# Moving projections, values and the first steps of cross attention between the eight units of a group

## The chip, the cores and the metric

The kernel runs on one core of a Trainium2 chip. The core has five engines, each with its own queue of instructions, which it works off in order: TensorE (PE, with its weight loads listed as PEld), VectorE (DVE), ScalarE (ACT), GpSimd (POOL) and SyncE (SP, which here only issues DMAs). They meet through semaphores alone. The metric is the device time of one execution in microseconds; the kernel before took 3197.55 us, the median of three runs (3197.34 to 3203.16).

## The reference

Input x is 64 sequences of 128 positions and 256 features in fp32, and so is a context. Two decoder layers run one after the other, each of three residual sublayers behind a layer normalization:

```
x = x + mamba(norm(x))                     layer 0: state space mixer
x = x + cross_attention(norm(x), context)  16 heads, rotary positions
x = x + recurrence(norm(x))                gated recurrence over the 64 sequences
x = x + self_attention(norm(x))            layer 1: 16 query heads, 4 key heads, RMS norm inside
x = x + cross_attention(norm(x), context)  one head 256 wide, no output projection
x = x + experts(norm(x))                   8 experts, 2 chosen per position, and a shared one
```

The change lies in the fourth and fifth lines. Self attention there is

```
q = (xn @ w_q) * rf;  k = (xn @ w_k) * rf;  v = xn @ w_v
s = softmax(q k^T / 16) v                  per head of 16
x = x + s + s @ w_o
```

and the cross attention is softmax((xn Wq + bq)(ctx Wk + bk)^T / 16) (ctx Wv + bv), one 128 x 128 score matrix for each sequence.

## The kernel before, in words

The 64 sequences stay in SBUF as 16 groups of four (X[g], 128 positions x 4 x 256). Four stages follow each other: layer 0's mixer; its cross attention with the recurrence; layer 1's two attentions with the routing of the experts; the experts. The change is in the third stage, which runs in the profile from about 1800 to 2735 us.

The order of that stage is written out. Each piece of work is a Python generator (`self_inputs`, `self_attention`, `cross_and_route`) and `run_units` (line 65) steps them: a step has a unit number and a priority, steps run by unit, then by priority, then by their place in the task list, and `yield du, p` says that the next step is du units later with priority p. The order in which steps emit instructions is the order in which PE, VectorE, ScalarE and GpSimd execute them (`manual_schedule(engines=PINNED)`); SyncE's DMAs are ordered by the framework. Units are no clock: a unit is only a stretch of each engine's queue, and an engine may be ahead of another.

One group takes eight units, and everything below repeats with that period, so a unit is known by its number modulo 8 (u0 to u7).

- **Self attention proper** (`attention`, line 241, priority 0 to 8 by step) has one step for each sequence b and half of the heads c, eight for a group, beginning at unit 8g+11. Two units after it begins PE makes the scores s (line 257, two matmuls on two halves of the array into the buffers s0 and s1), VectorE takes the minimum mx of each (L263), ScalarE makes the exponentials e with their sums (L275, four for s0, and at priority 4 four for s1). A unit later PE transposes e (pt, L287), ScalarE copies the first half to eT (L289) and VectorE the second (L291), and at priority 8 PE multiplies with the values (av, L305). After the second half of the heads follow, in odd units, the reciprocal sums (rd, L296 and L312), and in even units the copy prs (L317), their product oT (L320) and the output projection pr (L324), added to X by VectorE (L328) one unit on. The scores of half c wait until the exponentials have read that buffer in the unit before.
- **`self_inputs(g)`** begins at unit 8g, priority 5: load of the recurrence's output xo, addition (L739), tanh (L741), addition to X (L743, GpSimd), statistics (L194 to L198, their reciprocal root on GpSimd, L182), two factors (L749 to L754), the normalized xn on ScalarE (L208), its transposes (L220, copied to xnT by ScalarE, L222, and VectorE, L224), the three projections to q, q and k (L234, multiplied with the rotary factors by VectorE, L764) and the values pv (L242, copied by ScalarE, L774).
- **`cross_and_route(g)`** begins at unit 8g+24, priority 5: `wide_attention` is the cross attention: load of the context (L570), statistics, xn, values(0) of the first two sequences (L242, bias added by VectorE, L803), transposes, two projections (L234, copied by ScalarE, L815, with two products called junk on VectorE, L817), scores (L826), reductions (L830), values(2) of the other two sequences, exponentials (L838), transposes (L846), the copy eT2 (L848), the product po (L853) and its addition to X (L858). `route` follows one unit later: a third normalization (xnr), its transposes, two stores of xnT to DRAM (L872), the gate's logits pl (L242), ranks (L882 to L896), counts pc (L901) and places (L905 to L927), and eight indirect DMAs that scatter the rows (L931, GpSimd, priority 6).

Steps of priority 5 of three different groups share each unit with one step of attention. They stand after the attention's exponentials and before its pr and av.

PSUM has eight buffers of 128 x 512: one each for s0, s1, pt0, pt1 and av, and three ("mm") that all other matmul results take in turn. In SBUF xn and the context's tile have one buffer each (`xn` is shared by self and cross attention), xnT has two, q and k two.

Of the kernel before, what the change touches and what calls it, by code (L numbers as in the profile page):

```python
# [41 lines left out]
def mid(ap, n):  # L42

    return ap.unsqueeze(1).to_broadcast([ap.shape[0], n, ap.shape[1]])
# [34 lines left out]
def tile_decoder(ctx: ExitStack, tc: tile.TileContext, a: dict, out: bass.AP):  # L79
    nc = tc.nc  # L80
    B = a["x"].shape[0]
    NG = B // G
# [131 lines left out]
    def transposed(work, ps, xn, bufs=2):  # L214

        xnT = [work.tile([P, T], F32, tag=f"xnT{c}", name=f"xnT{c}", bufs=bufs) for c in range(2)]
        for c in range(2):
            pt = ps.tile([P, T], F32, tag="mm", name="pt_ln")
            for b in range(G):
                nc.tensor.transpose(pt[:, b * P:(b + 1) * P], xn[:, b, c * P:(c + 1) * P], ident)  # L220
            if c == 0:
                nc.scalar.copy(xnT[c], pt)  # L222
            else:
                nc.vector.tensor_copy(xnT[c], pt)  # L224
        return xnT

    def halves(t):
        return [t[:, c, :] for c in range(2)]
# [101 lines left out]
    def values_of(work, n, i):  # L330

        v = work.tile([P, n, 64], F32, tag=f"v{i}", name=f"v{i}")
        nc.gpsimd.memset(v[:, :, 16:48], 0.0)
        return v

    def pairs(v):

        return v.rearrange("p n (f e) -> p n f e", e=16)[:, :, 0:4:3, :]
# [194 lines left out]
    with phase_pool("work1", "left") as work, phase_pool("ps1", space=PSUM) as psp:  # L533
        ps = PsumPool(psp, {"mm": 6, "seg": 1})
        got = {}
# [21 lines left out]
    def scale_weights():  # L557
        nc.gpsimd.tensor_scalar_mul(fuo, fuo, 0.5)
        for c in range(2):
            for w in (lwq, lwk, lwv):  # L560
                nc.gpsimd.tensor_scalar_mul(w[:, c, :], w[:, c, :], lg[:, c:c + 1])

            wd = lwo[:, c, c * P:(c + 1) * P]
            nc.gpsimd.tensor_tensor(out=wd, in0=wd, in1=ident, op=ALU.add)
        nc.gpsimd.tensor_scalar_mul(lwq, lwq, -1.0 / 16)
        yield 1, 6
# [135 lines left out]
    with phase_pool("work2", "left") as work, phase_pool("ps2", space=PSUM) as psp:  # L702
        ps = PsumPool(psp, {"mm": 3, "s0": 1, "s1": 1, "pt0": 1, "pt1": 1, "av": 1})
        got = {"c2": c2, "v": [values_of(work, 8, i) for i in range(3)]}
        rows = [(g, b) for g in range(NG) for b in range(G)]
        tasks = [(40, 6, scale_weights())]
# [27 lines left out]
    ATTEND = 13  # L734

    def self_inputs(g, work, ps, hc, got):
        xo = work.tile([P, G, D], F32, tag="xo", name="xo")
        nc.sync.dma_start(out=xo, in_=XO[g])
        nc.gpsimd.tensor_tensor(out=xo, in0=xo, in1=mid(hc, G), op=ALU.add)  # L739
        yield 1, 5  # L740
        nc.scalar.activation(xo, xo, AF.Tanh)  # L741
        yield 1, 5
        nc.gpsimd.tensor_tensor(out=X[g], in0=X[g], in1=xo, op=ALU.add)  # L743
        yield 1, 5
        mv, rstd = start_norm(g, work)
        yield 1, 5

        ms = work.tile([P, G], F32, tag="ln_ms", name="ln_ms", bufs=2)
        nc.vector.tensor_tensor(ms, rstd, rstd, ALU.mult)  # L749
        nc.vector.tensor_tensor(ms, ms, mv[:, :, 1], ALU.mult)  # L750
        nc.vector.tensor_scalar(ms, ms, RMS_EPS, None, ALU.add)
        inv = power(work, "ln_inv", ms)
        yield 1, 5
        nc.vector.tensor_tensor(inv, inv, rstd, ALU.mult)  # L754
        xn = end_norm(g, work, mv, inv, "xn")
        yield 1, 5
        xnT = transposed(work, ps, xn)
        yield 1, 5
        qT = work.tile([P, 2, T], F32, tag="qT", name="qT", bufs=2)
        kT = work.tile([P, T], F32, tag="kT", name="kT", bufs=2)  # L760
        for c in range(3):
            pp = project(ps, lwq if c < 2 else lwk, c * P if c < 2 else 0, P, xnT)
            dst = qT[:, c, :] if c < 2 else kT
            nc.vector.tensor_tensor(  # L764
                dst.rearrange("p (b t) -> p b t", b=G), pp.rearrange("p (b t) -> p b t", b=G),
                mid(rfT, G), ALU.mult,
            )
            if c > 0:
                yield 1, 5
        pv = ps.tile([P, T], F32, tag="mm", name="pv")  # L770
        for b in range(G):
            project_rows(pv[:, b * 64:(b + 1) * 64], xnT, lwv, b)
        v = got["v"][g % 2]
        nc.scalar.copy(pairs(v), pv[:, :D].rearrange("p (n f e) -> p n f e", f=2, e=16))  # L774
        got[g] = qT, kT, v
# [15 lines left out]
    def wide_attention(g, work, ps):  # L791
        ctx_tile = load_ctx(work, g, 1)
        cT = halves(ctx_tile)
        mv, rstd = start_norm(g, work)
        yield 1, 5
        xn = end_norm(g, work, mv, rstd, "xn")
        v = work.tile([P, G, D], F32, tag="v2", name="v2")

        def values(b):
            pv = ps.tile([P, 2, D], F32, tag="mm", name="pv")  # L800
            for i in range(2):
                project_rows(pv[:, i, :], cT, ywv, b + i)
            nc.vector.tensor_tensor(v[:, b:b + 2, :], pv, mid(ybv, 2), ALU.add)  # L803

        values(0)
        yield 1, 5
        xnT = transposed(work, ps, xn)
        yield 1, 5
        qT = work.tile([P, 2, T], F32, tag="qT2", name="qT2")

        qb = work.tile([P, G], F32, tag="qb2", name="qb2", bufs=2)
        junk = work.tile([P, D], F32, tag="junk2", name="junk2")
        for c in range(2):
            pp = project(ps, ym, c * P, P, xnT)
            nc.scalar.activation(qT[:, c, :], pp, AF.Identity, bias=ymb[:, c:c + 1])  # L815
            for b in range(2 * c, 2 * c + 2):
                nc.vector.scalar_tensor_tensor(  # L817
                    junk, xn[:, b, :], 1.0, yu[:, :D], ALU.mult, ALU.mult, accum_out=qb[:, b:b + 1]
                )
            yield 1, 5  # L820
        nc.vector.tensor_scalar(qb, qb, yu[:, D:D + 1], None, ALU.add)
        s = ps.tile([P, G, P], F32, tag="mm", name="s")
        for b in range(G):
            tb = slice(b * P, (b + 1) * P)
            for k in range(2):
                nc.tensor.matmul(  # L826
                    s[:, b, :], lhsT=qT[:, k, tb], rhs=cT[k][:, tb], start=(k == 0), stop=(k == 1)
                )
        mx = work.tile([P, G], F32, tag="mx2", name="mx2", bufs=2)
        nc.vector.tensor_reduce(mx, s, AX.X, ALU.min)  # L830

        nc.vector.tensor_tensor(mx, mx, qb, ALU.add)
        nc.vector.tensor_tensor(mx, mx, qb, ALU.subtract)
        values(2)
        e = work.tile([P, G, P], F32, tag="e2", name="e2")
        den = work.tile([P, G], F32, tag="den2", name="den2", bufs=2)
        for b in range(G):
            nc.scalar.activation(  # L838
                e[:, b, :], s[:, b, :], AF.Exp, bias=mx[:, b:b + 1], scale=-1.0,
                accum_out=den[:, b:b + 1],  # L840
            )
        yield 2, 5
        nc.vector.reciprocal(den, den)
        pt = ps.tile([P, G, P], F32, tag="mm", name="pt")
        for b in range(G):
            nc.tensor.transpose(pt[:, b, :], e[:, b, :], ident)  # L846
        eT = work.tile([P, G, P], F32, tag="eT2", name="eT2")
        nc.scalar.copy(eT, pt)  # L848
        yield 1, 5
        for b in range(0, G, 2):  # L850
            po = ps.tile([P, 2, D], F32, tag="mm", name="po")
            for i in range(2):
                nc.tensor.matmul(  # L853
                    po[:, i, :], lhsT=eT[:, b + i, :], rhs=v[:, b + i, :], start=True, stop=True
                )
            for i in range(2):
                xb = X[g][:, b + i, :]
                nc.vector.scalar_tensor_tensor(  # L858
                    xb, po[:, i, :], den[:, b + i:b + i + 1], xb, ALU.mult, ALU.add
                )  # L860
        yield 1, 5
# [76 lines left out]
    def cross_and_route(g, work, ps, got):  # L938
        yield from wide_attention(g, work, ps)
        yield from route(g, work, ps, got)  # L940

    with phase_pool("work3", "left") as work, phase_pool("ps3", space=PSUM) as psp:
        ps = PsumPool(psp, {"mm": 3, "s0": 1, "s1": 1, "pt0": 1, "pt1": 1, "av": 1})
# [36 lines left out]
        nc.vector.tensor_tensor(hc, ph[:, :D], fbo, ALU.add)  # L980
        got = {"full": base, "v": [values_of(work, G * 2, i) for i in range(2)]}
        tasks = [(8 * g, 5, self_inputs(g, work, ps, hc, got)) for g in range(NG)]
        tasks += [(8 * g + ATTEND + 11, 5, cross_and_route(g, work, ps, got)) for g in range(NG)]
        tasks += [
            (8 * g + ATTEND - 2 + 2 * b + c, 0, self_attention(g, b, c, work, ps, got))
            for g in range(NG) for b in range(G) for c in range(2)
# [7 lines left out]
    with phase_pool("work4", "left") as work, phase_pool("ps4", space=PSUM) as psp:  # L994
        ps = PsumPool(psp, {"mm": 5, "dn": 3})
# [307 lines left out]
```

## Time and profile before

| | |
|---|---|
| median of three runs | 3197.55 us |
| the profiled execution | 3206.84 us, its span 3205.1 us |
| TensorE matmuls busy | 2996.5 us, 93% |
| TensorE weight loads busy | 2047.4 us, 64% |
| VectorE busy | 1972.3 us, 62% |
| ScalarE busy | 1861.5 us, 58% |
| GpSimd busy | 1262.5 us, 39% |
| granted TensorE clock, mean | 0.966 |
| from 1840 to 2680 us: PE, VectorE, ScalarE busy | 814.7, 619.5, 639.7 of 840 us |

How to read the lines that follow. A line of the timeline has the start in us, the length in us, the engine, the line of the code, the operation, what it writes and reads by the program's names, the tile's shape and how many instructions were merged; a bracket at its end tells how long the engine was idle before and what ended that. A fp32 matmul stands there as two instructions. Lengths of PE rows overlap, since a matmul's record runs on while the next is under way, so PE's pace is read from one start to the next. A line of the table by stretches has the stretch, its length, then the busy time of PE, PEld, VectorE, ScalarE and GpSimd with the number of instructions, the granted clock, the share of DMA and GB/s. The last line of the page's fourth part ranks engines by their share of the chain of waits that ended last.

### The profile page before, as it was taken

The page shows a single profiled execution, that of the slowest core. Times are in us where ns is not written, and L with a number is a line of the kernel's source. Part 1 is how long each engine was busy: PE and PEld are TensorE (multiplying, and loading weights), DVE is VectorE, ACT ScalarE, POOL GpSimd, SP SyncE. Part 2 cuts the span into 40 slices and gives each one's busy share as a digit, 9 for nine tenths or more (in the row PEclk, how much of TensorE's full clock was granted, in tenths as well). Part 3 has the DMA queues.
Part 4 walks back from the last instruction along what each step waited for, and adds up shares of the span by engine and source line. Part 5 has one row for each costly group of instructions (what it writes and reads, how often), then busy time and mean ns, then how long its engine had stood idle before and what let it go on. Part 6 is the DMA issues. An engine that isn't in the chain of part 4 may idle for free.

```text
span 3205.1 us, 54587 instructions
## 1 busy us (share of the span) xinstructions
PE 2996.5 (93%) x19022; PEld 2047.4 (64%) x19022; DVE 1972.3 (62%) x4955; ACT 1861.5 (58%) x6693; POOL 1262.5 (39%) x1204
## 2 busy tenths in 40 slices
PE   7999999996999999999999699999999997899587
PEld 4565555553777777777777456666666664688354
DVE  6887887773555555555555357777878774433344
ACT  4555555553777666766776377777787873233100
POOL 3444444453434433333332222434252422333564
PEclk9999999997999999999999899999999997899888
DMA  9990000001111111111110100111111111677453
GB/s 303 342 342 31 1 1 1 1 15 42 41 32 31 40 34 31 32 39 36 29 33 21 43 14 27 59 42 60 41 60 40 54 37 59 204 222 222 129 164 120
DMA packets 192196, 246.59 MB, mean 77 GB/s; under 512 B 24624, under 2 KB 156208, under 8 KB 191920
## 3 DMA queue, kind: packets, MB, share of 16 engines
q1 hardware_dynamic: 173952, 196.92, 19.9%
q0 software_dynamic: 17968, 46.18, 4.7%
q8 instruction: 150, 2.46, 0.3%
q14 instruction: 126, 1.03, 0.1%
HBM read 113.65 MB, written 127.93 MB: 75 GB/s over the span
## 4 chain that ended last, share of the span: by engine, by line
PE 75%; ACT 8%; DVE 6%; issue 4%; POOL 2%; another core or an unknown queue 1%; DMA 1%; SPq 1%; DVEq 0%; POOLq 0%; ACTq 0%
PE proj L234 18%; PE s L257 9%; PE pt L287 6%; PE pu L664 5%; PE pu L660 5%; PE av L305 4%; ACT e L275 3%; PE po L516 3%; PE seg L484 3%; PE pv L242 2%; PE pr L324 2%; PE pgu L1112 2%; PE py L501 2%; PE pxo L242 2%; PE pd L1175 2%
## 5 line engine op out<-in xcount | busy, mean ns | idle before, releaser
L275 ACT ACTIVATE e<-s,mx 128x128 f32<-128x128 f32 x2048 | 740.3, 395 | 384.6 <-DVE mx L263 384.6
L263 DVE TENSOR_REDUCE mx<-s 128x4 f32<-128x512 f32 x512 | 331.6, 685 | 465.2 <-PE s L257 455.3
L275 ACT ACTIVATION_READ_ACCUMULATOR e<-s,mx 128x1 f32 x2048 | 476.3, 233 | 0.0
L182 POOL TENSOR_TENSOR ln_rstd<-ln_ve,neghalf 128x4 f32<-128x4 f32 x80 | 82.1, 1026 | 685.2 <-DVE ln_ve L198 555.5
L257 PE MATMUL s<-kbd,qT 64*128 64x512 f32 x1024 | 334.5, 652 | 18.5 <-POOL qT L600 8.6
L287 PEld LDWEIGHTS pt<-consts,e 128*128 128x128 f32 x2048 | 223.0, 142 | 196.5 <-issue 151.0
L234 PE MATMUL proj<-xnT,win 128*128 128x512 f32 x640 | 298.9, 611 | 16.0 <-DVE xc L397 16.0
L287 PE MATMUL pt<-consts,e 128*128 128x128 f32 x2048 | 284.1, 282 | 0.0
L660 PE MATMUL pu<-xnTb,fx 128*128 128x128 f32 x1536 | 235.6, 276 | 1.2 <-DVE xnTb L651 1.2
L664 PE MATMUL pu<-c,fu 128*128 128x128 f32 x1536 | 234.5, 275 | 1.8 <-DVE c L695 1.8
L660 PEld LDWEIGHTS pu<-xnTb,fx 128*128 128x128 f32 x1536 | 208.0, 192 | 31.3 <-issue 23.9
L234 PEld LDWEIGHTS proj<-xnT,win 128*128 128x128 f32 x640 | 119.9, 194 | 147.7 <-issue 115.0
L407 DVE SCALAR_TENSOR_TENSOR acc<-proj,convw,acc 128x508 f32<-128x508 f32 (+2 forms) x288 | 207.0, 735 | 8.3 <-ACT acc L403 7.3
L342 POOL TENSOR_TENSOR kbd<-kT,consts 128x512 f32<-128x512 f32 x192 | 202.8, 1066 | 5.3 <-PE s L257 4.7
L664 PEld LDWEIGHTS pu<-c,fu 128*128 128x128 f32 x1536 | 202.3, 192 | 2.4 <-DVE c L695 2.4
L291 DVE COPY eT<-pt 128x512 f32<-128x512 f32 x256 | 174.9, 683 | 7.4 <-PE pt L287 7.4
L305 PE MATMUL av<-eT,v 128*32 128x128 f32 x4096 | 165.8, 280 | 13.3 <-ACT eT L289 13.3
L506 POOL TENSOR_TENSOR y<-y,zs 128x512 f32<-128x512 f32 x64 | 81.4, 1271 | 230.9 <-DVE y L505 223.1
L599 POOL TENSOR_TENSOR other<-other,consts 128x512 f32<-128x512 f32 x64 | 81.4, 1272 | 198.7 <-DMA other<-raw 198.7
L1136 POOL DMA_INDIRECT ys<-ys,t_yrow x128 | 124.7, 975 | 87.9 <-DVE x L1148 38.3
L305 PEld LDWEIGHTS av<-eT,v 128*32 128x32 f32 x4096 | 96.7, 109 | 96.1 <-issue 31.4
L289 ACT COPY eT<-pt 128x512 f32<-128x512 f32 x256 | 155.6, 608 | 2.9 <-PE pt L287 2.7
(277 smaller groups left out, 6432.4 us busy)
## 6 DMA issues: line engine op xcount, KB each, us to landing
xs<-zeros SPq DMA_DIRECT2D x64, 1024.0 KB
xs<-xs SPq DMA_DIRECT2D x71, 256.0 KB
ys<-y SPq DMA_DIRECT2D x71, 256.0 KB
ctxT<-in_ctxT_dram SPq DMA_DIRECT2D x32, 512.0 KB
other<-raw SPq DMA_DIRECT2D x256, 64.0 KB
x<-in_x_dram SPq DMA_DIRECT2D x16, 512.0 KB
xo<-xo SPq DMA_DIRECT2D x64, 128.0 KB
xo<-xo SPq DMA_DIRECT2D x16, 512.0 KB
```

The lines of the kernel that those rows point to most:

```text
L234: nc.tensor.matmul(o[:m, :], lhsT=w[:, k, m0:m0 + m], rhs=rhs[k], start=(k == 0), stop=(k == 1))
L257: nc.tensor.matmul(ss[i], lhsT=q()[rows], rhs=kb[rows, :, :], start=True, stop=True)
L263: nc.vector.tensor_reduce(mx[i], ss[i], AX.X, ALU.min)
L275: nc.scalar.activation(e[i][:, h, :], ss[i][:, h, :], AF.Exp, bias=mx[i][:, h:h + 1], scale=-1.0, accum_out=den[:, at:at + 1],)
L287: nc.tensor.transpose(pt[:, h, :], e[i][:, h, :], ident)
L289: nc.scalar.copy(eT[i], pt)
L291: nc.vector.tensor_copy(eT[i], pt)
L305: nc.tensor.matmul(av[j * 32:j * 32 + 32, c, :], lhsT=values(h), rhs=eT[h // 4][:, h % 4, :], start=(odd == 0), stop=(odd == 1),)
L342: nc.gpsimd.tensor_tensor(out=kb, in0=mid(k, 4), in1=last(mask, P), op=ALU.mult)
L407: nc.vector.scalar_tensor_tensor(acc[:, :, k:], pv[:, :, :P - k], convw[:, c, 3 - k:4 - k], acc[:, :, k:], ALU.mult, ALU.add,)
L660: nc.tensor.matmul(pu[:, i, :], lhsT=fx[:, k, m], rhs=xnT[:, k, :], start=(k == 0), stop=False)
L664: nc.tensor.matmul(pu[:, i, :], lhsT=fu[:, k, m], rhs=got["c2"][:, k, :], start=False, stop=(k == 1),)
```

## The change

Three things move; no operation is added or taken out.

- In `self_inputs` the first projection is followed by a step's end like the other two, so that the four pieces (three projections, values) lie in units 7, 8, 9 and 10 of the group; they lay in 7, 7, 8 and 9.
- In `wide_attention` values(0) stands behind the transposes of xn in the following unit; it stood in the unit of the normalization. values(2) stands in a unit of its own between the exponentials and the transposes of e; it stood before the exponentials, and the unit between had nothing of this piece.
- `cross_and_route` begins at unit 8g+25; it began at 8g+24. Its length in units is unchanged.

```diff
@@ self_inputs, in the loop over the three projections
-            if c > 0:
-                yield 1, 5
+            yield 1, 5
@@ wide_attention, after the normalization
+        yield 1, 5
+        xnT = transposed(work, ps, xn)
         values(0)
-        yield 1, 5
-        xnT = transposed(work, ps, xn)
         yield 1, 5
@@ wide_attention, after the reductions of the scores
-        values(2)
         e = work.tile([P, G, P], F32, tag="e2", name="e2")
         ...
-        yield 2, 5
+        yield 1, 5
+        values(2)
+        yield 1, 5
         nc.vector.reciprocal(den, den)
@@ the list of tasks
-        tasks += [(8 * g + ATTEND + 11, 5, cross_and_route(g, work, ps, got)) for g in range(NG)]
+        tasks += [(8 * g + ATTEND + 12, 5, cross_and_route(g, work, ps, got)) for g in range(NG)]
```

More of the change, by code (lines that the diff above doesn't have):

```diff
@@ L803, in values @@
             nc.vector.tensor_tensor(v[:, b:b + 2, :], pv, mid(ybv, 2), ALU.add)
-        values(0)
         yield 1, 5
         xnT = transposed(work, ps, xn)
+        values(0)
         yield 1, 5
```

## The prediction

> **What bounds the kernel now.** I read the page first (the chain that ended last), then busy time by unit, then each engine's order of work inside one group. On the chain TensorE has three quarters, so a gain has to come out of TensorE's own time.
>
> ```profile
> PE 75%; ACT 8%; DVE 6%; issue 4%; POOL 2%; another core or an unknown queue 1%; DMA 1%; SPq 1%; DVEq 0%; POOLq 0%; ACTq 0%
> ```
>
> The changed code repeats once a group. The context load, one a group, gives the period, 52.9 us; twelve groups (units 32 to 127) have it within 0.2 us.
>
> ```profile
> 2194.28 0.38 SPq L570 DMA_DIRECT2D ctxT<-in_ctxT_dram  x1
> 2247.16 0.38 SPq L570 DMA_DIRECT2D ctxT<-in_ctxT_dram  x1
> ```
>
> Busy time in the eight units of one group, cut where each unit's score matmuls start. I call them u1 to u7 and u0, unit number modulo 8, in the order of the rows.
>
> ```profile
> core 0: us, PE busy (x) PEld busy (x) DVE busy (x) ACT busy (x) POOL busy (x), PEclk, DMA share, GB/s
> 2162.55:2169.09 6.54, 6.54 (x58) 4.93 (x54) 6.42 (x26) 4.05 (x20) 2.64 (x3) 1.00 0.02 4
> 2169.09:2174.69 5.60, 5.15 (x41) 3.10 (x40) 3.77 (x6) 5.60 (x20) 4.93 (x5) 1.00 0.13 47
> 2174.69:2181.13 6.44, 6.44 (x46) 3.54 (x42) 5.45 (x17) 6.44 (x27) 3.56 (x4) 1.00 0.43 123
> 2181.13:2188.58 7.45, 7.45 (x53) 5.02 (x53) 4.12 (x16) 5.91 (x25) 5.42 (x6) 1.00 0.35 125
> 2188.58:2195.12 6.54, 6.54 (x58) 4.93 (x55) 5.13 (x12) 4.59 (x21) 4.39 (x4) 1.00 0.06 20
> 2195.12:2200.36 5.24, 4.73 (x42) 3.09 (x41) 3.70 (x9) 5.24 (x26) 0.00 (x0) 1.00 0.37 100
> 2200.36:2208.48 8.12, 8.12 (x50) 4.38 (x46) 6.36 (x19) 5.55 (x25) 0.00 (x0) 1.00 0.01 2
> 2208.48:2215.44 6.96, 6.96 (x45) 4.46 (x44) 6.21 (x23) 3.77 (x18) 0.00 (x0) 1.00 0.00 0
> ```
>
> PE looks full, but ScalarE is full in exactly the units u2, u3 and u6. The order inside shows what that costs:
>
> ```profile
> 2169.09 1.13 PE L257 MATMUL s<-kbd,qT 64*128 64x512 f32 x4
> 2171.97 0.77 PE L220 MATMUL pt_ln<-consts,xn 128*128 128x128 f32 x5 [0.16 <-ACT xn L208]
> 2174.12 0.64 PE L305 MATMUL av<-eT,v 128*32 128x128 f32 x16 [0.24 <-ACT eT L289]
> 2174.69 1.96 PE L257 MATMUL s<-kbd,qT 64*128 64x512 f32 x4
> ```
>
> The score matmuls use two halves of the array side by side and take 1.06 us from their start to the next group's. Where the second half waits for the last exponentials of the unit before, they run one after the other (1.96): +0.83, counted as busy. The reason is ScalarE's queue:
>
> ```profile
> 2168.85 1.11 ACT L741 ACTIVATE xo<-xo 128x1024 f32<-128x1024 f32 x1
> 2169.81 2.10 ACT L208 ACTIVATE xn<-x,ln_off,ln_rstd 128x256 f32<-128x256 f32 x4
> 2172.03 0.42 ACT L275 ACTIVATE e<-s,mx 128x128 f32<-128x128 f32 x1
> 2175.27 2.16 ACT L208 ACTIVATE xnr<-x,ln_off,ln_rstd 128x256 f32<-128x256 f32 x4
> ```
>
> In u1 a tanh and a normalization stand behind the exponentials, so those of u2 begin 2.94 us into their unit; in u1 they began 2.49 in, and with ScalarE and VectorE free it is 1.94 (u5: 2190.53 less 2188.58).
>
> **PE's own work per unit**, from start-to-start times of this group's PE timeline: scores 1.06, transposes of e 0.93, av 0.57; even units add pr 0.96, odd ones the transposes of rd 0.37. So 3.52 even, 2.93 odd. Inputs: a 512-column projection 1.72 to 1.80, pv of self attention 1.74, values 1.85, po 1.72, pl 1.71, cross scores 1.79, a normalized input's transposes 0.90, cross pt 0.56, pc 0.37.
>
> Before, u0 to u7: 6.96, 6.54, 4.40, 5.62, 7.03, 6.54, 4.45, 7.29; sum 48.83. Measured 52.89: **4.06 us a group are stall**, at u2 1.20, u3 0.83, u4 0.41, u6 0.79, u7 0.83. The largest gain is thus 12 x 4.06 = 49 us, some 54 with the partial groups.
>
> **The change, part by part.** No instruction is added or removed; matmuls, evacuations and DMAs stay as many. What counts is which unit each falls in.
>
> Self attention: the projections lie in u7, u0, u1 (were u7, u7, u0), pv in u2 (was u1). Cross attention and routing start one unit later; values(0) goes behind the transposes (now u3), values(2) behind the exponentials, a unit of its own (u7).
>
> PE after: u0 3.52+1.72+0.37+0.56 = 6.17; u1 2.93+1.72+1.72 = 6.37; u2 3.52+1.74 = 5.26; u3 2.93+0.90+1.85 = 5.68; u4 3.52+0.87+1.75 = 6.14; u5 2.93+1.71+1.80 = 6.44; u6 3.52+0.90+1.79 = 6.21; u7 2.93+1.72+1.85 = 6.50. Sum 48.8.
>
> ScalarE's inputs (tanh 0.96, a normalization 1.97, copy of xnT 0.47, qT 0.58, four cross exponentials 1.37, eT2 0.55, v 0.25): before 0, 3.18, 2.44, 1.05, 0.83, 3.34, 0.47, 0.55; after 0.55, 0.96, 2.22, 2.44, 1.05, 2.80, 1.84, 0. The two heaps of u1+u2 (5.62) and u5 (3.34) become 3.18 and 2.80. Its attention part is 3.24 even, 3.56 odd.
>
> VectorE, whole units: before 6.87, 4.70, 2.80, 5.45, 3.60, 4.20, 5.60, 6.00; after 5.25, 7.03, 3.96, 5.32, 4.11, 3.53, 3.71, 6.34. This is less even: po's adds 1.57, the cross statistics 1.79, the placing 0.79 and kT 0.61 all fall in u1, now only 6.37 long.
>
> Walking the units with these: exponentials start at the latest of 1.94 us, the first reduction + 0.78, and ScalarE's free time; the next unit starts after PE's work, and not before exponentials + 2.67 (even) or 3.04 (odd), since av waits for eT. For the kernel before this gives the rows above: u2 2.94 + 2.67 = 5.61 against 5.60. After: u7, u0 and u1 are PE's own work. In u1 VectorE starts its reductions at 1.16, works 2.27 + 4.76 and waits 0.5 for kT's projection, 8.66, so u2's first reduction starts at 2.29, the exponentials at 3.07, and u2 lasts 5.74 (**stall 0.48**). Its normalization ends ScalarE's work 2.79 into u3; scores serial 0.83, transposes wait 0.1: u3 lasts 6.61 (**stall 0.93**). ScalarE ends u3's exponentials at 6.35, before u4 begins, so u4 to u7 are PE's work. Sum 50.2: **-2.7 a group, -32 over twelve**.
>
> Edges: the two lighter groups at units 24 to 31 and 128 to 135 lose part of these stalls (-1.6, -2.4), units 16 to 23 -0.5. In the drain PE runs values(0) (2.71 there) behind the transposes and no longer while it waits for xn: +2; VectorE's ranking of the group before no longer stands behind the add of values(2): -2. The start of attention, 8g+11, is unmoved. Together -36.
>
> Costed at nothing, and what hides it. *ctxT*: its one buffer is free after values(2), now in u7 and not u5, and is read in u3. From the load's issue to values(0) that was 24.9 us (2166.28 + 52.9 less 2194.28) and becomes 0.9 + 6.17 + 6.37 + 5.74 + 3.8 = 23.0; the xo load queued behind it on SyncE waits for u2 anyway. Were 512 KB not there in 23 us, u3 would be longer by the lateness; no row shows such a wait. *xnT's two stores* go one unit later; nobody reads them before the last stage. *GpSimd*: the reciprocal root of the cross statistics now waits for u1's late VectorE and holds up the X addition (2.36), the routing root and the scatters behind it; the X addition then ends near 5.8 in u2 and is wanted 3.7 into u3, 3.6 us of cover. *xn's one buffer*: self's normalization (u5) must wait for the cross projection's last read of xn, on VectorE near 4.75 in u5; ScalarE gets there at 5.50, and u6 takes another 0.9 before PE feels it.
>
> Two rules of the Trainium skill speak against it. The row first:
>
> ```profile
> 2172.05 2.36 POOL L743 TENSOR_TENSOR x<-x,xo 128x1024 f32<-128x1024 f32 x1
> 2173.15 1.30 DVE L205 SCALAR_TENSOR_TENSOR ln_off<-ln_mv,ln_rstd 128x4 f32<-128x4 f32 x1
> ```
>
> A 0.15 us operation took 1.30 and ended with GpSimd's addition. "SBUF — State Buffer" (Who interferes with whom) says that a VectorE operation with two SBUF inputs and a GpSimd one that reads SBUF exclude each other for a whole instruction. By my walk the addition ends at 5.8 and the offset wants to run at 6.15: cost 0. By the rule with the addition a microsecond late, the offset slips to 6.9 and the normalization with it: +0.4 a group, +5 us. I take 0 and put the rest in the range. The other: "Perfetto Trace Analysis" (Identifying the Most-Contended Engine) says that regular bubbles can mean too little SBUF or PSUM for the next tile. u0, u4 and u6 now each ask four "mm" tiles of three buffers. The nearest row is u7 before, also four:
>
> ```profile
> 2206.98 0.63 PE L846 MATMUL pt<-consts,e 128*128 128x128 f32 x4
> ```
>
> It shows no wait. By that row the cost is 0, by the rule up to the third rival below; below nothing is excluded, as no tile is dropped. I take 0.
>
> **Rivals.** *All stalls go*: VectorE is in time for u2; 4.06 x 12 + 5: 3144 us. *They only move* (-6 to +6 us): u2's first reduction comes another 2.7 us late; for it speaks VectorE's 7.03 in u1, against it that its idle 2.0, 2.9 and 2.5 us in u4, u5 and u6 let it enter u7 without a backlog. *Slower, one mechanism*: in u0, u4 and u6 the buffer given to pr is one that ScalarE empties only after its exponentials (eT2 or xnT). pr then starts at 5.83, 6.15, 5.9 in place of 4.64, 4.61, 4.7: +4.05 a group, 54.2, +16 us, 3213. It decides once these waits exceed 2.7 a group. Against it: before, PE waited at pr for oT 31 times (12.4 us in all) and for junk 14 times (3.3), both on VectorE, never for a ScalarE copy. *It does not do what it says*: PE's shares do become even (4.4 to 7.3 becomes 5.3 to 6.5), VectorE's do not; that is the second rival.
>
> **The numbers.** Chances: my forecast 0.57, all stalls gone 0.13, moved 0.12, slower 0.18. The profiled execution took 3206.84 us (span 3205.1); 36 less is 3170.8. It is 9.3 above the median of the runs, 3197.55, which less 36 gives **3161**. The forecast's own range is 3148 to 3180 (a gain of 1.2 to 3.7 a group). The whole range, 3140 to 3206, holds the first three cases and leaves out most of the slower one. A difference under 0.2% (6.4 us) can't be told from none; faster by more is 0.57 + 0.13 + 0.03, within it 0.07, slower 0.02 + 0.18.
>
> **What would show it.** Right: a period of 50.2 between context loads; score matmuls of 1.96 us only in u3; ScalarE no longer full in u6; u7 6.5 and not 8.1. Wrong: pr starting 1 us late in u0, u4 or u6 with a bracket naming ScalarE; a first reduction in u2 later than 3 us; score matmuls serial in more units; a wait for ctxT.

## The result: 0.28% slower, with one unit of the eight 4 us longer

The changed kernel takes 3208.47 us (median of 13 runs, 3201.63 to 3212.72), the kernel before 3200.64 on the same chip (13 runs, 3188.55 to 3206.08): a ratio of 1.0028, 95% interval 1.0018 to 1.0037. The forecast was 3161, with a range that ended at 3206; the sign is wrong as well.

The profiled execution took 3211.52 us, its span 3209.7 (before 3206.84 and 3205.1). The page's fourth part, the shares of the chain that ended last, gives VectorE more than before (10%, was 6%):

```profile
PE 78%; DVE 10%; ACT 6%; issue 2%; another core or an unknown queue 2%; POOL 1%; DMA 1%; SPq 0%; DVEq 0%; ACTq 0%; POOLq 0%
```

The context loads in the timeline of the changed kernel give its period, 54.62 us where 50.2 was forecast and 52.89 was measured before:

```profile
2203.03 0.38 SPq L570 DMA_DIRECT2D ctxT<-in_ctxT_dram  x1
2257.65 0.38 SPq L570 DMA_DIRECT2D ctxT<-in_ctxT_dram  x1
```

The table by stretches of this group, cut where each unit's score matmuls start (u0 first, u7 last; the columns are those of the table of before):

```profile
2203.87:2210.16 6.29, 6.29 (x45) 3.81 (x45) 5.71 (x19) 4.24 (x19) 0.00 (x0) 1.00 0.30 83
2210.16:2216.63 6.47, 6.47 (x46) 3.90 (x43) 5.46 (x18) 4.52 (x19) 0.00 (x0) 1.00 0.00 1
2216.63:2222.16 5.53, 5.53 (x49) 4.04 (x49) 5.50 (x19) 3.09 (x16) 3.09 (x2) 1.00 0.02 4
2222.16:2228.62 6.46, 6.46 (x51) 4.31 (x47) 5.83 (x24) 6.46 (x29) 5.06 (x6) 1.00 0.40 122
2228.62:2235.25 6.63, 6.55 (x45) 3.90 (x44) 4.49 (x13) 6.63 (x27) 4.38 (x5) 1.00 0.22 79
2235.25:2241.78 6.53, 6.53 (x54) 4.17 (x50) 5.17 (x11) 4.25 (x19) 5.71 (x7) 1.00 0.35 123
2241.78:2252.02 10.24, 8.50 (x57) 6.14 (x56) 6.99 (x11) 6.93 (x26) 2.72 (x2) 0.83 0.00 1
2252.02:2258.49 6.47, 6.47 (x46) 3.90 (x42) 4.80 (x12) 5.06 (x26) 0.00 (x0) 1.00 0.01 3
```

Seven units lie within 0.5 us of the forecast (6.17, 6.37, 5.74, 6.61, 6.14, 6.44, and 6.50 for u7). **u6 takes 10.24 in place of 6.21**, and these 4.03 us are nearly the whole difference of 4.4 a group. It is the only unit with a granted clock under 1 (0.83) and the only one with a long gap in PE.

The timeline around the end of u5 shows what is late. VectorE, then GpSimd, ScalarE and PE:

```profile
2239.24 0.42 DVE L816 SCALAR_TENSOR_TENSOR junk<-xn,yu 128x256 f32<-128x256 f32 x1
2239.70 5.09 DVE L816 SCALAR_TENSOR_TENSOR junk<-xn,yu 128x256 f32<-128x256 f32 x1
2244.72 1.28 DVE L263 TENSOR_REDUCE mx<-s 128x4 f32<-128x512 f32 x2
...
2239.16 0.97 POOL L931 DMA_INDIRECT xs<-xnr,r_rows  x1 [0.30 <-issue]
2240.16 1.05 POOL L342 TENSOR_TENSOR kbd<-kT,consts 128x512 f32<-128x512 f32 x1
2241.15 2.35 POOL L739 TENSOR_TENSOR xo<-xo,hc 128x1024 f32<-128x1024 f32 x1
2243.46 1.03 POOL L342 TENSOR_TENSOR kbd<-kT,consts 128x512 f32<-128x512 f32 x1
...
2244.83 2.07 ACT L208 ACTIVATE xn<-x,ln_off,ln_inv 128x256 f32<-128x256 f32 x4 [3.94 <-DVE junk L816]
...
2245.48 0.33 PE L220 MATMUL pt_ln<-consts,xn 128*128 128x128 f32 x1 [1.55 <-ACT xn L208]
2245.97 2.31 PE L220 MATMUL pt_ln<-consts,xn 128*128 128x128 f32 x7 [0.16 <-ACT xn L208]
```

Two equal products follow each other. The first takes 0.42 us, the second 5.09: it ends at 2244.79, 0.30 us after a row of three GpSimd operations that stand without a gap (2240.16 to 2244.49). ScalarE's normalization for self attention writes the one buffer xn, which that product still reads, and so sits 3.94 us; PE waits for its result. The transposes and the cross scores behind them then run at a lower clock: 2.58 us for the scores (2248.08, L825) where a kernel below takes 1.95. The clock is a part of the loss of its own: a kernel below has the same hold and the same wait of PE, and there u6 takes 9.41 us in the groups where the clock stays at 1.00. By this estimate some 3.2 of the 4.03 us are the wait and some 0.8 the clock. u6's first reduction stands behind the product too, at 2244.72; 1.16 us into the unit, as in u5, would be 2242.94. The line of these products, in the changed kernel and in the one before, gives the whole count: 11 normalizations waited 40.0 us in all, and before no product took over 0.43 us.

```profile
L816 DVE SCALAR_TENSOR_TENSOR junk<-xn,yu x64: 415/421/5099, 1916.2 to 2702.3; 128x256 f32<-128x256 f32 x64
...
  ACT xn L208: 40.0, 11
```

```profile
L817 DVE SCALAR_TENSOR_TENSOR junk<-xn,yu x64: 415/422/427, 1919.8 to 2697.0; 128x256 f32<-128x256 f32 x64
```

The trace of the changed kernel has its own comparison. From u0's first reduction in one group to that in the next, ten groups with a product of 5.09 or 5.10 us take 54.5 to 54.7 us; the first group with all pieces, in which all four take 0.42, takes 49.85, and one with a product of 1.80 takes 50.57. The kernel before needs 52.7 to 52.9 in the same groups.

Why the two met only now is a matter of both queues. Before, the products of the second half stood in u4, and GpSimd's row began at the start of u5 (two kbd together at 2188.64, the addition of xo at 2190.64 to 2193.00, with u5 from 2188.58). Now the products stand in u5, 4.0 us into it; and the routing's indirect DMAs, also a unit later, stand between GpSimd's copies, so that its gapless row begins 4.9 us into u5.

### The profile page after: what moved, and what is told of

It is laid out like the page before. It is cut to its first block, busy times and chain, and to the rows that moved or that the text cites. A ratio compares the mean times of both kernels' runs of the same rounds, so it can differ in the third digit from the quotient of the medians.

```text
span 3209.7 us, 54546 instructions
## 1 busy us (share of the span) xinstructions
PE 2990.2 (93%) x19022; PEld 2046.6 (64%) x19022; DVE 2000.9 (62%) x4955; ACT 1860.3 (58%) x6693; POOL 1262.6 (39%) x1204
## 3 DMA queue, kind: packets, MB, share of 16 engines
q14 instruction: 126, 1.03, 0.1%
## 4 chain that ended last, share of the span: by engine, by line
PE 78%; DVE 10%; ACT 6%; issue 2%; another core or an unknown queue 2%; POOL 1%; DMA 1%; SPq 0%; DVEq 0%; ACTq 0%; POOLq 0%
PE proj L234 17%; PE s L257 7%; PE pt L287 6%; PE pu L664 5%; PE pu L660 5%; PE pgu L1112 4%; PE av L305 4%; PE po L516 3%; PE seg L484 3%; PE pr L324 3%; PE pv L242 3%; ACT e L275 2%; PE py L501 2%; PE pd L1121 2%
## 5 line engine op out<-in xcount | busy, mean ns | idle before, releaser
L182 POOL TENSOR_TENSOR ln_rstd<-ln_ve,neghalf 128x4 f32<-128x4 f32 x80 | 82.1, 1027 | 671.4 <-DVE ln_ve L198 622.5
L257 PE MATMUL s<-kbd,qT 64*128 64x512 f32 x1024 | 319.4, 649 | 14.5 <-POOL qT L600 8.6
```

The costliest lines, as they stand in the source:

```text
L257: nc.tensor.matmul(ss[i], lhsT=q()[rows], rhs=kb[rows, :, :], start=True, stop=True)
```

## The experiments

All eight kernels ran on one chip, where the kernel before took 3140.5 us (median of 16 runs beside the first four, 3140.7 of 7 runs beside the others). Its level is lower than that of the chip above, so only ratios are compared. The periods of the third stage are compared as they stand, since the granted clock is 1.00 in all eight units of a group in the kernel before there and in the first experiment here. A period here is the time from a group's first score reductions to the next group's.

**The theory** ("port and buffer"): a VectorE operation that reads two SBUF tensors is held while GpSimd works (the port); the one buffer xn passes the delay to ScalarE, and the queue of VectorE passes it to the reductions (the buffer). The rivals: the port alone or the buffer alone; that the hold comes from something else than the two inputs; and that another part of the change brings it.

### All four products in the step of the first projection

```diff
-            for b in range(2 * c, 2 * c + 2):
+            for b in range(G if c == 0 else 0):
```

> The changed kernel with all four products xn*yu (junk) in the step of the first cross projection, so that none of them lies in u5. Theory 'port and buffer' (the second product of u5 asks for VectorE's second SBUF input while GpSimd runs kbd, the xo addition and kbd without a gap, waits 4.7 us for them, and self attention's normalization on ScalarE waits for that product because xn has one buffer): no product longer than 0.43 us, period between context loads 50.0 to 50.8 us in place of 54.6, some 45 us less than the changed kernel, about 3163 us, ratio to the kernel before 0.985 to 0.991. If the loss lies elsewhere (VectorE's full u1, a PSUM buffer for pr): period still 54, about 3208 us.

Measured: 3107.11 us, ratio 0.9893 (0.9879 to 0.9908). Periods 50.42 to 50.58, and no product over 0.43 us in these groups. As expected: the only thing moved are two 0.42 us operations, from u5 to u4, and the group loses 4.1 us. GpSimd's row of three stands there as before; nothing of two SBUF inputs is in its way.

### A buffer of its own for the cross attention's xn

```diff
-        xn = end_norm(g, work, mv, rstd, "xn")
+        xn = end_norm(g, work, mv, rstd, "xn2")
```

Two small tiles (junk and bk) share buffers with others here, to make the room.

> The changed kernel with a buffer of its own for cross attention's xn; the products stay in u5 (two scratch tiles share buffers with others of their size to make room). Theory 'port and buffer': the second product of u5 still takes 5.1 us, but ScalarE starts self's normalization at about 5.5 us into u5; VectorE's reductions of u6 begin at 2.9 us into the unit and not at 1.16, so u6 lasts 6.4 and u7's scores run serially: period about 51.3 us, about 3175 us. Rival 'buffer alone' (the product's length is only a record, the order on ScalarE is what costs): period 50.2, 3160 us. Rival 'port alone' (what costs is VectorE standing still, not the buffer): period 54 to 55, 3208 us.

Measured: 3120.64 us, ratio 0.9935 (0.9921 to 0.9949), periods 51.67 to 51.82. The product is still held 5.09 us, but ScalarE no longer waits for it. What is left stands in the timeline of this kernel, VectorE and PE in u6:

```profile
2227.26 5.09 DVE L816 SCALAR_TENSOR_TENSOR junk<-xn,yu 128x256 f32<-128x256 f32 x1
2234.42 0.68 DVE L224 COPY xnT<-pt_ln 128x512 f32<-128x512 f32 x1
...
2235.15 1.13 PE L324 MATMUL pr<-lwo,oT 128*128 128x256 f32 x4 [0.98 <-DVE xnT L224]
```

VectorE comes late to everything behind the product, and pr, the fourth tile of u6 for three PSUM buffers, waits 0.98 us for the copy of xnT. The granted clock in this u6 is 1.00. So of the 4.1 us the buffer carries 2.8 (54.6 to 51.8), the lower clock of u6 included, and VectorE's own queue 1.2 (51.8 to 50.57). Neither rival alone fits.

### Without the addition of hc on GpSimd

```diff
-        nc.gpsimd.tensor_tensor(out=xo, in0=xo, in1=mid(hc, G), op=ALU.add)
```

This kernel leaves out the term hc in xo.

> The changed kernel without GpSimd's addition of hc to xo (2.35 us a group); this leaves out the term of the recurrence's last state, tanh reads xo as loaded. Theory 'port and buffer': GpSimd's gapless run shrinks from 4.4 to 2.1 us, the second product of u5 takes 2.7 us in place of 5.1, u6 lasts 7.9 in place of 10.2, period 52.3 us, about 3183 us. Rival 'buffer alone': the product still 5.1 us, period 54.6, 3208 us.

Measured: 3098.59 us, ratio 0.9863 (0.9849 to 0.9878), periods 50.40 to 50.56, the product 1.79 us. The size was missed: a hold of 2.7 was expected. VectorE and GpSimd in the timeline of this kernel:

```profile
2162.72 1.79 DVE L815 SCALAR_TENSOR_TENSOR junk<-xn,yu 128x256 f32<-128x256 f32 x1
...
2163.16 1.06 POOL L342 TENSOR_TENSOR kbd<-kT,consts 128x512 f32<-128x512 f32 x1
2166.12 1.04 POOL L342 TENSOR_TENSOR kbd<-kT,consts 128x512 f32<-128x512 f32 x1 [1.90 <-PE s L257]
```

Without the addition the second copy does not follow at once; it waits for PE. The product ends 0.29 us after the first copy does (2164.51 against 2164.22). With the gap in GpSimd's queue it is held by one operation, without it by three. A hold of 1.79 costs the group nothing: 50.4 to 50.56 is the period of the kernel without any hold.

### The second half's products with one SBUF input

```diff
-                nc.vector.scalar_tensor_tensor(
-                    junk, xn[:, b, :], 1.0, yu[:, :D], ALU.mult, ALU.mult, accum_out=qb[:, b:b + 1]
-                )
+                if c == 0:
+                    nc.vector.scalar_tensor_tensor(
+                        junk, xn[:, b, :], 1.0, yu[:, :D], ALU.mult, ALU.mult, accum_out=qb[:, b:b + 1]
+                    )
+                else:
+                    nc.vector.tensor_reduce(qb[:, b:b + 1], xn[:, b, :], AX.X, ALU.add)
```

This kernel leaves out the factor yu in the second half's products.

> The changed kernel, with the two products of the second half replaced by plain sums of xn (the factor yu is left out of these two, so they read one SBUF tensor instead of two); same place in the queue, same wait, same one buffer xn. Theory (two SBUF inputs and GpSimd exclude each other): the sums take under 0.5 us each, self's normalization is not held up, 50.2 to 50.8 us a group, ratio 0.984 to 0.991. Rival (what holds the product is its place behind something else, or GpSimd's traffic slows any VectorE operation that reads SBUF): the second sum still ends with GpSimd's second block-diagonal copy, 54 to 55 us a group, ratio about 1.003.

Measured: 3104.23 us, ratio 0.9888 (0.9872 to 0.9905), periods 50.41 to 50.57. The timeline, VectorE (the two sums stand in one row) and GpSimd:

```profile
2221.17 0.73 DVE L821 TENSOR_REDUCE qb<-xn 128x1 f32<-128x256 f32 x2
...
2222.08 1.05 POOL L342 TENSOR_TENSOR kbd<-kT,consts 128x512 f32<-128x512 f32 x1
2223.08 2.36 POOL L739 TENSOR_TENSOR xo<-xo,hc 128x1024 f32<-128x1024 f32 x1
2225.39 1.04 POOL L342 TENSOR_TENSOR kbd<-kT,consts 128x512 f32<-128x512 f32 x1
```

Place, wait and buffer are those of the changed kernel, GpSimd's row is there without a gap, and the hold is gone. That fits the two inputs and not the rival that the place in the queue does it. One reserve: the pair of sums is some 0.2 us shorter than the pair of products (0.73 against 0.88 or more), and ends 0.18 before the first copy's record begins. So it didn't meet GpSimd's row itself. The trace of the kernel before has the missing case, though. In the rows of it shown further on, the addition of pr to X (L328, 128 x 256 like the products, one input in PSUM and one in SBUF) begins inside GpSimd's addition of xo and takes its usual 0.42 us; 0.7 us behind it an operation with two SBUF inputs (L754) is held until the end of that addition.

Two more places show where the theory as worded above is too wide. In u4 of the changed kernel both products of the first half begin inside the reciprocal root on GpSimd (L182), which reads SBUF too, and take 0.41 and 0.42 us. GpSimd, then the first of the two on VectorE:

```profile
2233.06 1.04 POOL L182 TENSOR_TENSOR ln_inv<-ln_ms,neghalf 128x4 f32<-128x4 f32 x1 [1.55 <-DVE ln_ms L751]
...
2233.48 0.41 DVE L816 SCALAR_TENSOR_TENSOR junk<-xn,yu 128x256 f32<-128x256 f32 x1
```

The GpSimd operations that held have 512 or 1024 elements in a partition, this one 4; whether that is the reason isn't shown. And a row without a gap need not hold to its end. In the kernel of the first experiment one of the lighter groups at the start of the stage has two products inside such a row (VectorE, then GpSimd):

```profile
1959.74 1.14 DVE L816 SCALAR_TENSOR_TENSOR junk<-xn,yu 128x256 f32<-128x256 f32 x1
1960.92 1.14 DVE L816 SCALAR_TENSOR_TENSOR junk<-xn,yu 128x256 f32<-128x256 f32 x1
...
1959.36 2.41 POOL L342 TENSOR_TENSOR kbd<-kT,consts 128x512 f32<-128x512 f32 x2
1961.73 2.53 POOL L739 TENSOR_TENSOR xo<-xo,hc 128x1024 f32<-128x1024 f32 x1
```

Each of them waits for one GpSimd operation and then runs ahead of the next, which becomes longer instead (2.41 us for two copies where 2.04 is usual, 2.53 for the addition where 2.36 is). These two begin while a GpSimd operation is under way; the product held 5.09 us begins 0.46 ahead of the row. Why that makes the difference stays open.

### Each part of the change alone

Self attention's part alone: a step's end after every projection, everything else as before.

```diff
-            if c > 0:
-                yield 1, 5
+            yield 1, 5
```

> The kernel before with the first part of the change alone: one self projection a unit (u7, u0, u1) and the values in u2; cross attention and routing as before. By the unit tables: PE's work becomes 6.96, 6.52, 6.14, 5.62, 7.03, 6.54, 4.45, 5.57 for u0 to u7; u2 is then long enough for ScalarE, u4, u6 and u7 keep 0.7, 0.8 and 0.8 of stall: period about 51.2 us, some 20 us faster than the kernel before, ratio 0.993. xn is read last in u4, so the products meet no gapless run of GpSimd: all 0.42 us under 'port and buffer'. Rival (the first part brings the loss): period above 53.

Measured: 3150.32 us, ratio 1.0027 (1.0018 to 1.0036), most periods 54.1 to 54.4: a miss, and of the wrong sign. The products take 0.42 us here in all groups but one near the end (1.83), so it is another place. VectorE, GpSimd and PE in u2 of this kernel:

```profile
2169.67 2.18 DVE L205 SCALAR_TENSOR_TENSOR ln_off<-ln_mv,ln_rstd 128x4 f32<-128x4 f32 x1
2171.78 0.68 DVE L224 COPY xnT<-pt_ln 128x512 f32<-128x512 f32 x1
...
2169.45 2.37 POOL L743 TENSOR_TENSOR x<-x,xo 128x1024 f32<-128x1024 f32 x1
...
2169.55 1.04 PE L220 MATMUL pt_ln<-consts,xn 128*128 128x128 f32 x8
2172.51 1.13 PE L324 MATMUL pr<-lwo,oT 128*128 128x256 f32 x4 [1.91 <-DVE xnT L224]
```

The same hold on another operation: the offset of a normalization, 0.15 us of work, stands 2.18 us until GpSimd's addition to X ends (2171.82). The copy of xnT behind it comes late, and pr, the fourth "mm" tile of a unit that now has self attention's values besides the cross attention's transposes, waits 1.91 us for the buffer. A lower clock follows, as in u6 of the changed kernel. u3 of this group and u3 of the next, in the table by stretches:

```profile
2174.29:2181.34 7.05, 7.05 (x46) 3.94 (x42) 4.90 (x16) 4.55 (x21) 1.67 (x2) 0.78 0.18 72
2228.30:2233.99 5.69, 5.69 (x46) 3.28 (x43) 4.50 (x15) 4.30 (x21) 1.39 (x3) 1.00 0.26 104
```

In both groups pr waits 1.9 us, but only in the first does the clock fall. Nine of eleven groups are like the first; the two others have a period of 52.65 in place of 54.1 to 54.4. So the miss of 3 us a group is 1.5 us of hold and buffers against the expected 51.2, and 1.5 of clock.

To part the hold from the buffers, the same kernel without GpSimd's addition; it leaves out adding xo to X.

```diff
-        nc.gpsimd.tensor_tensor(out=X[g], in0=X[g], in1=xo, op=ALU.add)
```

> Self attention's part of the change alone, and GpSimd's addition of xo to X (2.37 us) left out, with the rest of the step. With the addition, the offset of the cross normalization was held 2.18 us, the copy of xnT behind it came late and pr waited 1.91 us in u2 for that copy's PSUM buffer. Theory (the hold is the cause, the four tiles of three buffers only pass it on): the offset takes under 0.3 us, pr waits under 0.4 us, 51.2 to 52.4 us a group (54.2 with the addition), ratio 0.987 to 0.995. Rival (the PSUM buffers alone): pr still waits more than 1 us, 53.5 to 54.2 us a group, ratio 0.999 to 1.003.

Measured: 3114.63 us, ratio 0.9925 (0.9908 to 0.9941), periods 51.52 to 51.54. VectorE and PE in u2:

```profile
2145.23 0.15 DVE L205 SCALAR_TENSOR_TENSOR ln_off<-ln_mv,ln_rstd 128x4 f32<-128x4 f32 x1
2146.20 0.69 DVE L224 COPY xnT<-pt_ln 128x512 f32<-128x512 f32 x1 [0.82 <-PE pt_ln L220]
...
2146.95 1.13 PE L324 MATMUL pr<-lwo,oT 128*128 128x256 f32 x4 [0.79 <-DVE xnT L224]
```

The offset takes 0.15, and the period falls by 2.7, as the theory has it: 1.1 against the two groups at full clock, and 1.5 as the clock no longer falls (it is 1.00 in every unit of the steady groups). But pr still waits 0.79 us, where under 0.4 was expected: VectorE now starts the copy as soon as PE has written the tile, and pr waits for it all the same. So of the 1.91 us the hold made 1.1; 0.8 stay without it, since pr still waits for one of the three buffers.

The cross attention's part alone: its start one unit later, values(0) behind the transposes, values(2) in its own unit; self attention as before.

> The cross attention's part of the change without self attention's. By the unit tables of the prediction u7 keeps two projections and gets values(2) (8.2 us) and u2 is left with 3.5 us of PE work in a unit that ScalarE makes 5.6 long: 51.8 us a group if nothing is held. Theory (a VectorE operation with two SBUF inputs is held while GpSimd works, and self's normalization waits for the product through the one buffer xn): the products of the second half lie in u5 as in the changed kernel and meet the same GpSimd work, so one of them takes about 5 us and the group about 55 us, ratio 1.006 to 1.012. Rival (self attention's part brings the block): all products 0.42 us, 51.8 us a group, ratio 0.994 to 0.998.

Measured: 3162.72 us, ratio 1.0075 (1.0058 to 1.0093), as expected; periods 54.95, 55.87 and 56.46 in turn; the second product of the second half takes 5.08 or 5.09 us in ten groups. The timeline, VectorE and ScalarE:

```profile
2248.61 5.09 DVE L817 SCALAR_TENSOR_TENSOR junk<-xn,yu 128x256 f32<-128x256 f32 x1
...
2253.75 2.07 ACT L208 ACTIVATE xn<-x,ln_off,ln_inv 128x256 f32<-128x256 f32 x4 [3.93 <-DVE junk L817]
```

So the hold comes with the cross attention's part. It is not needed that the projections move. The three periods differ by the clock of u6. The second u6 below is that of the group of the rows above; PE waits 1.54 us for the normalization in both:

```profile
2194.83:2205.16 10.33, 8.46 (x58) 6.20 (x57) 6.98 (x11) 6.94 (x26) 2.71 (x2) 0.83 0.00 0
2250.70:2260.11 9.41, 7.38 (x57) 5.01 (x57) 6.99 (x11) 6.36 (x25) 2.71 (x2) 1.00 0.00 1
```

### A version with the products early and the statistics one unit earlier

The kernel of the first experiment, and the cross attention's statistics in u0 (its task begins a unit earlier and its first step's end counts two units).

```diff
         mv, rstd = start_norm(g, work)
-        yield 1, 5
+        yield 2, 5
...
-        tasks += [(8 * g + ATTEND + 12, 5, cross_and_route(g, work, ps, got)) for g in range(NG)]
+        tasks += [(8 * g + ATTEND + 11, 5, cross_and_route(g, work, ps, got)) for g in range(NG)]
```

> The kernel with all four products in the step of the first projection, and besides the cross attention's statistics (1.79 us of VectorE) one unit earlier, in u0 instead of u1. Theory (the rest of the stall, 0.48 in u2 and 0.93 in u3 by the prediction's walk, comes from VectorE's 7.0 us in u1): u2's first reduction starts near 1.2 us into its unit instead of 2.2, the score matmuls of u3 take 1.1 us and not 1.96, 48.8 to 49.5 us a group, ratio 0.978 to 0.986. Rival (another two-input operation of VectorE falls under a GpSimd operation in the new order, or u0 becomes VectorE's): 50.4 us a group or more, ratio 0.989 or above.

Measured: 3100.46 us, ratio 0.9871 (0.9855 to 0.9888), periods 49.95. By the ratios it beats the kernel before and the changed one. The period fell by 0.6 where 1.1 to 1.8 was expected, and the ratio is just outside what was. u3's score matmuls run side by side again (1.13), and u3 takes 5.70 in place of 6.46. But u2 takes 5.87 in place of 5.53, since its own score matmuls now stretch (the timeline, PE):

```profile
2196.78 1.70 PE L257 MATMUL s<-kbd,qT 64*128 64x512 f32 x4
```

Part of the stall moved one unit back. u2's first reduction does not start near 1.2 us into its unit either, but at 2198.02, 1.24 after the unit's start: that part came as expected. The ratio's interval overlaps that of the first experiment, so by the ratios the step between these two versions isn't settled; by the period it is 0.6 us a group, and all four runs (up to 3101.49) lie below all four of that kernel (from 3106.30).

## Why the prediction was wrong

**The step that failed** is the last of "Costed at nothing": *xn's one buffer*. It said that VectorE is done with xn near 4.75 us into u5, ScalarE gets there at 5.50, and u6 takes another 0.9 before PE feels it. The place was right: the product begins 4.45 into u5 (2239.70 less 2235.25) and at its usual length would have been done at 4.87. It was done at 9.54. The cover was 1.6 us, the lateness 4.7, so 3 us or more had to reach PE. u6 lost 4.03; the 0.8 or so beyond the wait stand with the lower clock, for which the prediction had no term at all. The step named the wait and its price without asking what might make the operation in front of it longer.

**The rule that was weighed in the wrong place.** The prediction quoted "SBUF — State Buffer" (Who interferes with whom) and a row of 1.30 us for it, then applied it to one operation, the offset in u2, and took 0. In u2 that was right: the offset takes 0.15 us in the steady groups after. The rule had to be asked of every VectorE operation with two SBUF inputs that the change moves, against every GpSimd operation near its new place. The trace of before showed the row that was needed. VectorE and GpSimd in its u5:

```profile
2190.95 0.42 DVE L328 TENSOR_TENSOR x<-pr,x 128x256 f32<-128x256 f32 x1
2192.03 1.00 DVE L754 TENSOR_TENSOR ln_inv<-ln_inv,ln_rstd 128x4 f32<-128x4 f32 x1
...
2188.64 2.04 POOL L342 TENSOR_TENSOR kbd<-kT,consts 128x512 f32<-128x512 f32 x2
2190.64 2.36 POOL L739 TENSOR_TENSOR xo<-xo,hc 128x1024 f32<-128x1024 f32 x1
```

A 0.1 us operation in u5 ends at 2193.03, with the addition of xo at 2193.00; and 4.4 us of GpSimd stand there without a gap. Moving the products into that unit puts their cost between 0 and 4.4 us or so, and with no cover beyond 1.6 the sum would have reached from -2.7 to about 0 a group (-2.7 + 4.4 - 1.6). Read as a hold by one GpSimd instruction for its whole length, the page's sentence gives at most 2.36 here: 0.7 past the cover, and still a gain. The trace showed 5.09, through three of them, and none at all through the reciprocal root; the measurement decides.

**The GpSimd step was incomplete.** It followed the reciprocal root, the addition to X and "the scatters behind it", but didn't write down where u5's kbd copies and the addition of xo go once the scatters stand a unit later. The addition went from 2.1 to 5.9 us into u5, with a copy directly before it and one directly behind, onto the products.

**The rival for the slower side** had the wrong mechanism for the changed kernel. It put the loss in pr waiting for a buffer emptied by ScalarE in u0, u4 and u6, +4.05 a group. No PE row of pr has a gap in the group shown, and nearly all of the loss is in one unit. Only in u4 does its weight load wait (2233.62, 0.91 us, for VectorE's copy of xnT), which costs PE some 0.2: from proj's start to pr's are 1.96 us, the forecast had 1.75. The 4.05 are besides 0.12 more than the three delays add up to. That the rival's period (54.2) and time (3213) come close to the measured ones is chance. The second rule, of bubbles that mean too little PSUM ("Perfetto Trace Analysis" has it under Optimization Strategy, not under the section that the prediction names), wasn't idle, though: pr waited 1.91, 0.98 and 0.79 us in three of the experiments, each time for VectorE's copy.

**What held.** The unit tables. With the hold taken away, the kernel of the first experiment runs u0 to u7 in 6.29, 6.47, 5.53, 6.46, 6.63, 6.53, 6.18 and 6.47 us, against the forecast's 6.17, 6.37, 5.74, 6.61, 6.14, 6.44, 6.21 and 6.50: 50.57 against 50.2, so the -2.7 a group was -2.3. The term most off is u4, 0.49. Its score matmuls take 0.18 more than the 1.06 of the sum (a row of 1.31 us in place of 1.13): ScalarE reads the last exponentials' sums until 0.13 after u4 begins, and the walk had it done before. pr starts 0.20 late, as above, and takes 0.11 more than its 0.96. In the changed kernel too u2's first reduction is where it was forecast (2218.83, 2.20 into the unit; 2.29 forecast), serial score matmuls of 1.96 stand in u3 alone, u7 takes 6.47, and no wait for ctxT appears.

**The sum.** Ten groups that are 4.1 us longer than the first experiment's period, by the hold and the clock, make +41 us; the forecast's -36 becomes +5. Measured were +7.8 between the medians and +4.6 between the spans. The 0.37 a group by which the tables were off make another 4 over twelve groups. How the rest divides between the partial groups and the other stages wasn't followed up.

## What to carry to other kernels

When steps move in a hand-ordered schedule, list for each moved VectorE operation how many SBUF tensors it reads, and lay GpSimd's queue beside it at the new place, with all that stands without a gap: the length of that row, not of one operation, bounds the cost in the runs here, though it need not be reached. An operation far longer in one row of the profile than in its others (1.00 where 0.10 is usual) is a sign of such a meeting already there, even where it costs nothing. A wait of PE can cost more than its length: here some 0.8 us came on top where the granted clock fell behind it. A move that evens out one engine's work can be right to within 1% of its unit table and still lose, if a shared buffer ties the next unit to an operation that can be held; here two operations of 0.42 us, one unit earlier, turned +0.28% into -1.07% (on two chips, each against the kernel before).

## What the runs showed of the hardware

- A fp32 VectorE product with two SBUF inputs (0.42 us) was held 5.09 us, through three GpSimd operations in a row (1.05, 2.35 and 1.03 us). VectorE did not get in between them there; where GpSimd paused after the first (1.90 us), the product was done 0.29 us later. Two products that began inside a row were each held for one operation only (1.14 us), and GpSimd's next became 0.2 us longer.
- The hold was seen only on operations with two inputs in SBUF: an operation of the same shape with one in PSUM and one in SBUF took its usual 0.42 us inside GpSimd's addition of 2.36. And not every GpSimd operation holds: inside its 128 x 4 root of 1.04 us the product took 0.41 to 0.43.
- The held product's record begins 0.46 us before that of the first GpSimd operation, and by its usual length would have ended at 2240.12, with GpSimd's beginning at 2240.16. An indirect DMA on GpSimd's queue is under way until 2240.13. Which side comes first can't be read from the starts of the records.
- GpSimd's indirect DMAs did not hold: the first product ran in its 0.42 us while one of 0.97 us was under way (2239.16 to 2240.13).
- The hold came back in every steady group: ten running of 5.09 or 5.10 us with a period of 54.6 us, and ten of 5.08 to 5.10 with one of 51.8 (the kernel with two buffers for xn).
- The granted clock fell in the third stage's steady groups only right after PE had stood still for 1.5 us or more: to 0.83 in u6 in all ten groups of the changed kernel (1.54 to 1.56 us), in seven of ten with the cross attention's part alone (1.54), and in nine of eleven with self attention's alone (1.9 to 2.1). Beside groups at full clock it cost some 0.8 to 1.6 us each time. After gaps up to 1.26 us it stayed at 1.00. What decides it where the gaps are alike isn't shown.
